# Adding gathered rows in pairs within their buffer, and ordering strided writes by stripe, in a recommendation model's kernel

## The chip, the core and the metric

The kernel runs on one core of a Trainium2 chip. The core has five engines, each with its own queue of instructions: TensorE (PE in the profile, its weight loads PEld), VectorE (DVE), ScalarE (ACT), GpSimd (POOL) and SyncE (SP, which here only issues DMAs). They run side by side and are ordered against one another by semaphores. Data lies in SBUF and PSUM on the core, both with 128 partitions, and in HBM outside it. The metric is the device time of one execution in microseconds (us); lower is better.

## The reference

The model scores 16384 rows. For each row it averages 32 word embeddings of 300 numbers and three sets of 20 embeddings of 64 numbers, looks up four single embeddings, puts all of it side by side (748 numbers) and sends it through three layers and a sigmoid. A "wide" sum of one number for each small lookup is added before the sigmoid.

```python
tok = word_emb[token_idx].mean(axis=1)          # 50000 x 300, 32 lookups a row
e1 = emb_mh1[mh1_idx].mean(axis=1)              # 1000 x 64, 20 lookups
e2 = emb_mh2[mh2_idx].mean(axis=1)              # 5000 x 64, 20 lookups
e3 = emb_mh3[mh3_idx].mean(axis=1)              # 10000 x 64, 20 lookups
o1, o2, o3, o4 = emb_oh1[oh1_idx], emb_oh2[oh2_idx], emb_oh3[oh3_idx], emb_oh4[oh4_idx]
emb = concatenate([tok, e1, e2, e3, o1, o2, o3, o4], axis=1)
wide = ...                                      # sum of one number of each of the 64 small lookups
h = relu(emb @ W1 + b1)                         # 748 -> 1024
h = relu(h @ W2 + b2)                           # -> 512
h = relu(h @ W3 + b3)                           # -> 256
return sigmoid(h @ Wd + bd + wide)
```

## The kernel before

The 16384 rows are 128 tiles of 128 rows, one row to a partition. Three kinds of work are done for each tile.

**Token rows.** The word table stays in HBM. For each of a tile's 32 tokens GpSimd issues one indirect DMA (`gather`, line 220) that fetches 128 rows of 300 floats. Two gathers fill one buffer of the ring `tok_rows` (`TOK_GROUP` = 2, `TOK_BUFS` = 3), and such a group of two rows is added up by VectorE two groups later (`TOK_LAG` = 2). `add_up` (line 525) does it: the first group of a tile (q = 0) is one add of the two rows `a` and `b` into `tok_sum`, 300 columns of the PSUM bank `own`; each of the other 15 groups is two adds, first `a` to `tok_sum`, then `b`. The last add of a tile writes to the tile's feature row in SBUF, `g`, in place of `tok_sum`. The generator `tokens` (line 538) issues the gathers of one group and the adds of an earlier one in one go. A gather into a buffer waits until both of its rows have been added.

**Small tables.** These are done as counting and matrix products. For 6 positions at a time, 11 steps for a tile, VectorE compares keys to numbers and writes one-hot rows (`one_hots`, line 599, tile `hot`), of which ScalarE scales one part in place; TensorE multiplies them into counts in PSUM (`counts`, line 616, tile `pc`), and ScalarE evicts the counts into the tile `cnt`. An eviction writes for each of 138 table slices the 6 positions of its step, so that the 11 evictions of a tile write interleaved columns of `cnt`, a stripe each. In the next tile's steps TensorE multiplies `cnt` by the tables (`small_sums`, line 639, tile `pg`), and VectorE reduces the result into `g`.

**Layers.** Each tile's `g` is transposed by TensorE and scaled into `x` by VectorE; four tiles at a time go through the layers (`mlp`, line 798), in 32-bit floats, and ScalarE applies bias and ReLU.

The order of the work is written by hand in the loop over `n_steps` = 128 x 11 + 27 steps. Each step issues the next one-hots, the counts, a share of the small sums, the tokens due by `tokens_by` (a steady pace, some 1.4 groups a step) and a share of the layers. Every engine takes its instructions in that order.

**How waits come about.** No instruction is sent to an engine directly. `Queue` and `Program.record` (line 146) note for each one which parts of which tiles it reads and writes (`region`, line 137: first and last partition, first and last byte of a row), find the earlier instructions whose regions overlap where one of the two writes, and keep of these the last for each stream (an engine's queue, or a DMA lane). An instruction of the same engine counts too, other than on TensorE. What is known to be done already by way of an earlier wait is dropped. `emit` (line 231) then sends all of it out: one wait rides on the instruction itself, and further ones become instructions of their own, issued ahead of it (line 247). A write takes out of the list those earlier accesses that lie wholly within its region. Line 98 is where all engine calls are recorded, so that nearly every instruction bears that line, and line 222 is the gather.

A region is one span of bytes. Two evictions that write interleaved columns of `cnt` overlap as spans though they share no byte, so that each one waits for the one before it.

Of the kernel before, what the change touches and what calls it, by code (L numbers as in the profile page):

```python
# [62 lines left out]
TOK_AT = 7 * ROW  # L63
WIDE_AT = COLUMN["o4"]
G_COLS = TOK_AT + TOK_D
# [38 lines left out]
class Program:  # L104
# [31 lines left out]
    @staticmethod  # L136
    def region(ap):
        size = SIZES[ap.dtype]
        pitch = size_of(ap.tensor)
        at = int(ap.offset) * size  # L140
        p0, b0 = divmod(at, pitch)
        dims = [(int(step), int(n)) for step, n in ap.ap]
        span = sum((n - 1) * abs(step) for step, n in dims[1:])
        return p0, p0 + dims[0][1], b0, b0 + (span + 1) * size

    def record(self, emit, sequencer, stream, reads, writes, clear=(), batch=None):
        ins = Instruction(emit, sequencer, self.stream(stream))
        if batch is not None:
            batch.append(ins)
            ins.batch = batch  # L150
        needed = {}

        def need(other):
            other = other.batch[-1]
            if other.batch is ins.batch:
                return
            if other.stream == ins.stream and stream == "PE":
                return
            best = needed.get(other.stream)
            if best is None or best.tick < other.tick:  # L160
                needed[other.stream] = other

        regions = [(self.region(ap), ap.tensor.name, False) for ap in reads if on_chip(ap)]
        regions += [(self.region(ap), ap.tensor.name, True) for ap in writes if on_chip(ap)]
        for (p0, p1, b0, b1), name, write in regions:
            for (q0, q1, c0, c1, wrote, _), other in self.accesses.get(name, {}).items():
                if (write or wrote) and p0 < q1 and q0 < p1 and b0 < c1 and c0 < b1:
                    need(other)
            if name in self.taken and not write and sequencer != "PE":
                banks, bank = self.taken.pop(name)  # L170
                banks.free.append(bank)
        for other in clear:
            need(other)
        known = self.known[sequencer]
        waits = [o for s, o in needed.items() if known.get(s, 0) < o.tick]
        waits = [
            o
            for o in waits
            if not any(d is not o and d.knows(o.stream) >= o.tick for d in waits)
        ]  # L180
        if waits:
            known = dict(known)
            for o in waits:
                for s, tick in o.known.items():
                    if known.get(s, 0) < tick:
                        known[s] = tick
                known[o.stream] = max(known.get(o.stream, 0), o.tick)
                o.signals = True
            self.known[sequencer] = known
        ins.waits = waits  # L190
        self.ticks[ins.stream] += 1
        ins.tick = self.ticks[ins.stream]
        ins.known = known
        self.members[ins.stream].append(ins)
        for region, name, write in regions:
            p0, p1, b0, b1 = region
            held = self.accesses.setdefault(name, {})
            if write:
                for key in [
                    k for k in held if p0 <= k[0] and k[1] <= p1 and b0 <= k[2] and k[3] <= b1  # L200
                ]:
                    if held[key] is not ins:
                        del held[key]
        for region, name, write in regions:
            self.accesses[name][(*region, write, ins.stream)] = ins
        self.program.append(ins)
        return ins
# [62 lines left out]
def size_of(tensor):  # L270
    n = 1
    for d in list(tensor.shape)[1:]:
        n *= int(d)
    return n * SIZES[tensor.dtype]


def on_chip(ap):
    return ap.space in (bass.MemoryType.SB, bass.MemoryType.PSUM)
# [37 lines left out]
def kernel(  # L316
# [21 lines left out]
    nc = tc.nc  # L338
# [8 lines left out]
    for f in SMALL:  # L347
        n = -(-tables[f].shape[0] // P)
# [4 lines left out]
    core, nc = nc, program  # L353
# [59 lines left out]
    tok_sum = own[:, 128 : 128 + TOK_D]  # L413
# [9 lines left out]
    at = 0  # L423
# [90 lines left out]
    def features(t):  # L514
        if t not in g_of:
            g_of[t] = gp.next()
        return g_of[t]

    tiles_all = B // P
    n_groups = N_TOK // TOK_GROUP  # L520
    n_all = B // P * n_groups + TOK_LAG
    summed = set()
    token_indices = {}

    def add_up(t, q, rows):

        a, b = rows
        if q == 0:
            nc.vector.tensor_add(tok_sum, a, b)
        else:  # L530
            nc.vector.tensor_add(tok_sum, tok_sum, a)
            to = tok_sum
            if q == n_groups - 1:
                to = features(t)[:, TOK_AT:G_COLS]
                summed.add(t)
            nc.vector.tensor_add(to, tok_sum, b)

    def tokens():

        under_way = []  # L540
        for n in range(n_all):
            if n < n_all - TOK_LAG:
                t, q = divmod(n, n_groups)
                it = token_indices[t // NSUB][:, t % NSUB, :].bitcast(U32)
                tok_rows, batch = tokp.next(), []
                rows = []
                for r in range(TOK_GROUP):
                    j = q * TOK_GROUP + r
                    rows.append(tok_rows[:, r * TOK_D : (r + 1) * TOK_D])
                    program.gather(f"gather{tokp.slot}", rows[-1], word, it[:, j : j + 1], batch, tok_rows)  # L550
                under_way.append((t, q, rows))
            if n >= TOK_LAG:
                add_up(*under_way.pop(0))
            yield 1
# [373 lines left out]
    for step in range(n_steps):  # L928
        t, i = divmod(step, STEPS)
# [29 lines left out]
        if waiting and step >= waiting[0][0]:  # L959
            _, k, ks = waiting[0]  # L960
# [91 lines left out]
```

## Time and profile before

| | before |
|---|---|
| median of 3 runs | 6906.27 us (6901.63 to 6929.64) |
| the profiled execution, by itself | 6980.96 us |
| its span, first to last instruction | 6979.1 us |
| mean granted TensorE clock | 0.882 |
| TensorE matmul busy | 5500.9 us (79%) |
| GpSimd busy | 3887.4 us (56%) |
| VectorE busy | 3573.1 us (51%) |
| ScalarE busy | 2698.0 us (39%) |

Busy times are unions of an engine's instructions. Ends of matmuls are modelled, so TensorE's busy share says little on its own. Rows name an instruction by engine, operation and tiles as out<-in, with buffer numbers left out: `own<-own,tok_rows` is an add of a gathered row to the token sum, `cnt<-pc` a count eviction, `hot<-own,sc` the making of one-hots (the numbers to compare with lie in the bank `own` too), `tok_rows<-in_word_emb_dram,it` a gather. "[5.48 <-DVE own]" behind a row is idle time of its engine ahead of it and what ended it. "remote" or "another core or an unknown queue" stands where a semaphore rose and no instruction that the profile shows ended just before; "issue" where nothing was waited for.

### The profile page before, as it was taken

The page shows a single profiled execution, that of the slowest core. Times are in us where ns is not written, and L with a number is a line of the kernel's source. Part 1 is how long each engine was busy: PE and PEld are TensorE (multiplying, and loading weights), DVE is VectorE, ACT ScalarE, POOL GpSimd, SP SyncE. Part 2 cuts the span into 40 slices and gives each one's busy share as a digit, 9 for nine tenths or more (in the row PEclk, how much of TensorE's full clock was granted, in tenths as well). Part 3 has the DMA queues.
Part 4 walks back from the last instruction along what each step waited for, and adds up shares of the span by engine and source line. Part 5 has one row for each costly group of instructions (what it writes and reads, how often), then busy time and mean ns, then how long its engine had stood idle before and what let it go on. Part 6 is the DMA issues. An engine that isn't in the chain of part 4 may idle for free.

```text
span 6979.1 us, 84734 instructions
## 1 busy us (share of the span) xinstructions
PE 5500.9 (79%) x33626; PEld 3574.2 (51%) x33626; DVE 3573.1 (51%) x6612; ACT 2698.0 (39%) x3433; POOL 3887.4 (56%) x4103
## 2 busy tenths in 40 slices
PE   5577888878878878878878878877877887777887
PEld 3455555455455545555545545544444544444666
DVE  4555555555555555555555555555555555555541
ACT  4343433333333433343333433333333333333331
POOL 5555555555555555555555555555555555555553
PEclk8789888888989889989888988898888988889888
DMA  5333333333333333333333333333333333333331
GB/s 157 95 95 93 93 97 94 91 92 92 96 93 94 93 92 93 93 94 93 93 92 94 94 93 93 92 92 92 91 93 91 94 93 92 93 91 95 89 86 50
DMA packets 253077, 651.47 MB, mean 93 GB/s; under 512 B 119195, under 2 KB 119835, under 8 KB 252679
## 3 DMA queue, kind: packets, MB, share of 16 engines
q0 software_dynamic: 196608, 629.41, 33.4%
q1 hardware_dynamic: 56071, 16.65, 1.1%
q8 instruction: 262, 4.29, 0.3%
q14 instruction: 136, 1.11, 0.1%
HBM read 645.59 MB, written 0.07 MB: 93 GB/s over the span
## 4 chain that ended last, share of the span: by engine, by line
PE 48%; another core or an unknown queue 17%; DVE 15%; issue 14%; ACT 3%; DMA 2%; POOL 1%; DVEq 0%; SPq 0%; POOLq 0%
PE ph L98 21%; PE pg L98 19%; PE pc L98 8%; DVE own L98 7%; DVE hot L98 6%; DMA tok_rows<-in_word_emb_dram,it 2%; DVE g L98 1%; POOL tok_rows L222 1%; ACT cnt L98 1%; ACT hot L98 1%; ACT odd L98 0%; DVE keys L98 0%; DVE x L98 0%; DVE ix L98 0%
## 5 line engine op out<-in xcount | busy, mean ns | idle before, releaser
L222 POOL DMA_INDIRECT tok_rows<-in_word_emb_dram,it x4096 | 3886.5, 949 | 3009.8 <-DVE own L98 1930.3
L98 PE MATMUL pg<-terms,cnt 128*128 128x195 bf16 x17664 | 2030.6, 268 | 562.3 <-issue 352.8
L98 PEld LDWEIGHTS pg<-terms,cnt 128*128 128x128 fp8e3 x17664 | 1681.7, 106 | 850.3 <-issue 528.6
L98 DVE TENSOR_TENSOR own<-own,tok_rows 128x300 f32<-128x300 f32 x3712 | 1766.3, 476 | 583.8 <-DMA tok_rows<-in_word_emb_dram,it 457.0
L98 ACT ACTIVATE cnt<-pc 128x828 uint16<-128x828 f32 (+1 forms) x1408 | 1187.7, 844 | 1909.6 <-remote 1152.1
L98 ACT ACTIVATE hot<-hot 64x768 bf16<-64x768 bf16 (+1 forms) x1408 | 1155.2, 820 | 1780.5 <-DVE hot L98 1495.3
L98 DVE TENSOR_TENSOR hot<-own,sc 128x1656 bf16<-128x1656 bf16 (+1 forms) x1408 | 1389.0, 987 | 861.4 <-remote 531.6
L98 PE MATMUL ph<-x,w_sb 128*128 128x512 f32 (+5 forms) x3492 | 1594.9, 587 | 69.5 <-issue 34.7
L98 PEld LDWEIGHTS pc<-hot 128*128 128x128 bf16 x8192 | 622.6, 102 | 1200.5 <-issue 793.5
L98 PE MATMUL pc<-hot 128*128 128x138 bf16 x8192 | 814.2, 233 | 457.4 <-ACT hot L98 215.0
L98 PE MATMUL ph<-odd,w_sb 128*128 128x512 f32 (+2 forms) x2368 | 1061.4, 576 | 44.4 <-issue 33.7
L98 DVE TENSOR_REDUCE g<-pg 128x130 f32<-128x390 f32 (+1 forms) x512 | 260.7, 509 | 1493.2 <-remote 971.3
L98 PEld LDWEIGHTS ph<-x,w_sb 128*128 128x128 f32 (+1 forms) x3492 | 635.5, 207 | 497.6 <-issue 443.2
L98 PEld LDWEIGHTS ph<-odd,w_sb 128*128 128x128 f32 x2368 | 422.7, 204 | 313.9 <-issue 297.7
L98 PE MATMUL pc<-ident,g 128*128 128x128 f32 x762 | 150.2, 345 | 262.6 <-ACT cnt L98 188.5
L98 ACT ACTIVATE odd<-ph,b_sb 128x512 f32<-128x512 f32 (+2 forms) x365 | 231.0, 633 | 294.0 <-remote 168.1
L98 PE MATMUL ph<-even,w_sb 128*128 128x512 f32 (+2 forms) x592 | 263.7, 573 | 23.8 <-issue 16.4
L98 PEld LDWEIGHTS pc<-ident,g 128*128 128x128 f32 x762 | 111.3, 177 | 286.5 <-ACT cnt L98 207.2
L98 DVE TENSOR_TENSOR x<-pc,scale 128x768 f32<-128x768 f32 x127 | 120.8, 951 | 158.7 <-PE pc L98 88.6
L98 ACT ACTIVATE even<-ph,b_sb 128x512 f32<-128x512 f32 (+2 forms) x148 | 93.1, 630 | 170.3 <-remote 104.7
L98 PEld LDWEIGHTS ph<-even,w_sb 128*128 128x128 f32 x592 | 107.4, 205 | 98.4 <-issue 84.6
L98 DVE COPY sc<-pc 128x512 bf16<-128x512 bf16 x64 | 44.1, 690 | 175.2 <-PE pc L98 141.8
(50 smaller groups left out, 552.7 us busy)
## 6 DMA issues: line engine op xcount, KB each, us to landing
tok_rows<-in_word_emb_dram,it POOLq DMA_INDIRECT x4096
ix<-in_idx_dram SPq DMA_DIRECT2D x64, 64.0 KB
w_sb<-in_W_dram SPq DMA_DIRECT2D x6, 512.0 KB
it<-in_idx_dram SPq DMA_DIRECT2D x64, 32.0 KB
w_sb<-in_W_dram SPq DMA_DIRECT2D x1, 2048.0 KB
odd<-in_mh_dram SPq DMA_DIRECT2D x3, 682.5 KB
even<-in_mh_dram SPq DMA_DIRECT2D x1, 682.5 KB
out_dram<-x SPq DMA_DIRECT2D x29, 2.0 KB
```

What stands on the lines that cost most here:

```text
L98: lambda: call(*args, **operands), self.name, self.name, aps + list(named.values()), outs
L222: return self.nc.gpsimd.indirect_dma_start(out=out, out_offset=None, in_=table, in_offset=bass.IndirectOffsetOnAxis(ap=index, axis=0),)
```

## The change

`add_up` forms the pair's sum first: for q > 0 the rows of a group are added in place, `a = a + b` within the gathered buffer in SBUF, and then `a` is added to `tok_sum`. It is still two adds a group. The choice of the place that the last add writes to (`to`) moves up.

`region` also gives a stripe, where an access has more than one free dimension: the period of the outermost one and the bytes within a period that the access touches. In `record`, two accesses whose stripes have the same period and no common byte (`apart`) aren't ordered against each other. A write takes an earlier access off the list only if its own stripe covers it (`covers`). An access in one unbroken piece has no stripe and is treated as before.

```diff
--- before.py
+++ after.py
@@ -141,7 +141,23 @@
         p0, b0 = divmod(at, pitch)
         dims = [(int(step), int(n)) for step, n in ap.ap]
         span = sum((n - 1) * abs(step) for step, n in dims[1:])
-        return p0, p0 + dims[0][1], b0, b0 + (span + 1) * size
+        stripe = (0, 0, 0)
+        free = [(step, n) for step, n in dims[1:] if n > 1]
+        if len(free) > 1 and all(step > 0 for step, _ in free):
+            outer = max(free)
+            width = 1 + sum((n - 1) * step for step, n in free if (step, n) != outer)
+            at = b0 % (outer[0] * size)
+            if at + width * size <= outer[0] * size:
+                stripe = (outer[0] * size, at, at + width * size)
+        return p0, p0 + dims[0][1], b0, b0 + (span + 1) * size, stripe
+
+    @staticmethod
+    def apart(one, other):
+        return one[0] == other[0] > 0 and (one[2] <= other[1] or other[2] <= one[1])
+
+    @staticmethod
+    def covers(one, other):
+        return not one[0] or one[0] == other[0] and one[1] <= other[1] and other[2] <= one[2]
 
     def record(self, emit, sequencer, stream, reads, writes, clear=(), batch=None):
         ins = Instruction(emit, sequencer, self.stream(stream))
@@ -162,10 +178,11 @@
 
         regions = [(self.region(ap), ap.tensor.name, False) for ap in reads if on_chip(ap)]
         regions += [(self.region(ap), ap.tensor.name, True) for ap in writes if on_chip(ap)]
-        for (p0, p1, b0, b1), name, write in regions:
-            for (q0, q1, c0, c1, wrote, _), other in self.accesses.get(name, {}).items():
+        for (p0, p1, b0, b1, one), name, write in regions:
+            for (q0, q1, c0, c1, two, wrote, _), other in self.accesses.get(name, {}).items():
                 if (write or wrote) and p0 < q1 and q0 < p1 and b0 < c1 and c0 < b1:
-                    need(other)
+                    if not self.apart(one, two):
+                        need(other)
             if name in self.taken and not write and sequencer != "PE":
                 banks, bank = self.taken.pop(name)
                 banks.free.append(bank)
@@ -193,11 +210,14 @@
         ins.known = known
         self.members[ins.stream].append(ins)
         for region, name, write in regions:
-            p0, p1, b0, b1 = region
+            p0, p1, b0, b1, stripe = region
             held = self.accesses.setdefault(name, {})
             if write:
                 for key in [
-                    k for k in held if p0 <= k[0] and k[1] <= p1 and b0 <= k[2] and k[3] <= b1
+                    k
+                    for k in held
+                    if p0 <= k[0] and k[1] <= p1 and b0 <= k[2] and k[3] <= b1
+                    and self.covers(stripe, k[4])
                 ]:
                     if held[key] is not ins:
                         del held[key]
@@ -525,15 +545,15 @@
     def add_up(t, q, rows):
 
         a, b = rows
+        to = tok_sum
+        if q == n_groups - 1:
+            to = features(t)[:, TOK_AT:G_COLS]
+            summed.add(t)
         if q == 0:
-            nc.vector.tensor_add(tok_sum, a, b)
+            nc.vector.tensor_add(to, a, b)
         else:
-            nc.vector.tensor_add(tok_sum, tok_sum, a)
-            to = tok_sum
-            if q == n_groups - 1:
-                to = features(t)[:, TOK_AT:G_COLS]
-                summed.add(t)
-            nc.vector.tensor_add(to, tok_sum, b)
+            nc.vector.tensor_add(a, a, b)
+            nc.vector.tensor_add(to, tok_sum, a)
 
     def tokens():
```

## The prediction

> **What bounds the kernel now.** The page comes first: the busy line says whether one engine sets the pace, the chain line whose work ended last.
>
> ```profile
> span 6979.1 us, 84734 instructions
> ...
> PE 5500.9 (79%) x33626; PEld 3574.2 (51%) x33626; DVE 3573.1 (51%) x6612; ACT 2698.0 (39%) x3433; POOL 3887.4 (56%) x4103
> ...
> PE 48%; another core or an unknown queue 17%; DVE 15%; issue 14%; ACT 3%; DMA 2%; POOL 1%; DVEq 0%; SPq 0%; POOLq 0%
> PE ph L98 21%; PE pg L98 19%; PE pc L98 8%; DVE own L98 7%; DVE hot L98 6%; DMA tok_rows<-in_word_emb_dram,it 2%; DVE g L98 1%; POOL tok_rows L222 1%; ACT cnt L98 1%; ACT hot L98 1%; ACT odd L98 0%; DVE keys L98 0%; DVE x L98 0%; DVE ix L98
> ```
>
> No engine is full. The chain is half TensorE, and VectorE, the engine that the change touches most, has 15% of it; the token adds (own) have 7%. ScalarE's count evictions (cnt) have 1%. The timeline of a short stretch in the middle shows how the engines take turns.
>
> ```profile
> 3495.79 0.41 PE L98 MATMUL pc<-hot 128*128 128x138 bf16 x4
> ...
> 3497.24 0.22 PE L98 MATMUL pc<-hot 128*128 128x138 bf16 x1 [1.05 <-issue]
> ...
> 3497.95 0.23 PE L98 MATMUL pc<-hot 128*128 128x138 bf16 x1 [0.49 <-issue]
> 3500.78 0.86 ACT L98 ACTIVATE cnt<-pc 128x828 uint16<-128x828 f32 x1 [6.47 <-remote]
> 3500.94 0.56 DVE L98 TENSOR_REDUCE g<-pg 128x130 f32<-128x390 f32 x1 [7.32 <-remote]
> 3501.42 1.01 DVE L98 TENSOR_TENSOR hot<-own,sc 128x1656 bf16<-128x1656 bf16 x1
> ...
> 3502.35 2.01 DVE L98 TENSOR_TENSOR own<-own,tok_rows 128x300 f32<-128x300 f32 x4
> ...
> 3503.60 0.95 POOL L222 DMA_INDIRECT tok_rows<-in_word_emb_dram,it  x1 [5.48 <-DVE own L98]
> ...
> 3504.26 0.95 DVE L98 TENSOR_TENSOR x<-pc,scale 128x768 f32<-128x768 f32 x1
> ```
>
> TensorE comes to a crawl at 3495.79 (single matmuls, 0.7 us and more apart, that wait for nothing shown), ScalarE and VectorE stand idle for 6 to 7 us, GpSimd runs out of row buffers and waits 5.48 us. Then VectorE works off its arrears without a pause: reduce, one-hot, two groups of adds, evictions. The change does nothing for the first phase. It can only shorten the second, and only where TensorE is short of what VectorE makes. These two views price both sides of that:
>
> ```profile
> L98 DVE TENSOR_TENSOR own<-own,tok_rows 128x300 f32<-128x300 f32 x3712 | 1766.3, 476 | 583.8 <-DMA tok_rows<-in_word_emb_dram,it 457.0 <-issue 44.8 <-DVE hot L98 4.5
> L98 DVE TENSOR_TENSOR hot<-own,sc 128x1656 bf16<-128x1656 bf16 (+1 forms) x1408 | 1389.0, 987 | 861.4 <-remote 531.6 <-PE pc L98 281.4 <-issue 19.9
> ...
> L98 DVE TENSOR_TENSOR own<-tok_rows 128x300 f32<-128x300 f32 x128 | 60.7, 474 | 38.3 <-DMA tok_rows<-in_word_emb_dram,it 31.9 <-issue 3.6 <-DVE g L98 0.4
> L98 DVE TENSOR_TENSOR g<-own,tok_rows 128x300 f32<-128x300 f32 x128 | 60.2, 470 | 4.4
> ```
> ```profile
> POOL tok_rows L222 <- DVE own L98: 1930.3, 1019, 20.4
> ...
> DVE own L98 <- DMA tok_rows<-in_word_emb_dram,it: 488.9, 459, 3.8
> ```
>
> Adds busy: 1766.3 + 60.7 + 60.2 = 1887 us. On the chain they have 7% of 6979 us, 489 us. So about 489/1887 = 26% of what an add costs is on the path: the share by which I weigh savings on VectorE.
>
> **The change part by part.** *Waits that go.* The standalone waits of the program all stand under line 247:
>
> ```profile
> L247 DVEq EVENT_SEMAPHORE  x1886: 21/21/21, 13.1 to 6900.0; - x189
> L247 ACTq EVENT_SEMAPHORE  x1096: 17/17/38, 9.9 to 6766.5; - x183
> ```
>
> A group's first add needs its gather and the add before it, two semaphores, so one wait is an instruction of its own. The new pair add reads only the gathered buffer and needs the gather alone; the second add needs the pair add alone (same engine, later tick). So up to 15 of 16 groups x 128 tiles = 1920 lose a wait; nearly all of VectorE's 1886 fit that. The other 128 (q = 0) keep theirs. Mostly the sequencer does such a wait while VectorE still runs the instruction before it: the one-hot ends at 3501.42 + 1.01 = 3502.43 and the adds behind it begin at 3502.35, 0.08 us earlier. There the 21 ns cost nothing. They show where VectorE has run dry and waits for a landing, as in the chain in order of time:
>
> ```profile
> 3508.55 0.47 DVE own L98
> 3509.02 0.03 issue
> 3509.05 0.48 DVE own L98
> 3509.53 0.67 issue
> 3510.20 0.02 DVEq L247
> 3510.22 0.04 issue
> 3510.26 0.49 DVE own L98
> 3510.75 0.02 issue
> 3510.78 0.48 DVE own L98
> ```
>
> From the end of the standalone wait's own time to the add it is 0.06 us, where an add that holds its wait follows 0.02 to 0.03 us behind its releaser. So 0.04 us for each of 459 landings waited for: 18 us of VectorE.
>
> *The order of dependence.* Before, every add depends on the one in front, also from group to group: 0.03 us between them. In the four adds of 2.01 us that is 4 x 0.476 = 1.90 plus three gaps of 0.03. After, the first add of a group is independent of the add before it, and an independent instruction starts early: 0.08 us before the end (one-hot to adds), 0.10 us (adds to x: 3502.35 + 2.01 = 3504.36 against 3504.26). Each place where two groups follow directly gains 0.03 + 0.09 = 0.12 us. How many such places? 2048 groups and 1408 one-hots, so at least 640 groups have no one-hot in front; some of these, up to 459, waited for a landing instead. Between 181 and 640; I take 400, near the middle: 400 x 0.12 = 48 us (22 to 77). Inside a group the second add still depends on the first: 0.03 us, as now.
>
> By the Trainium skill (VectorE: DVE Perf Modes, The DRAIN you can't avoid) the next operation doesn't start until the pipe is empty, and in a chain of copies semaphores between them cost nothing extra; these 48 us would be nil. The two overlaps above speak against its use here (the section allows that operations which aren't held start earlier).
>
> *The add itself.* Out of PSUM into PSUM 476 ns; two rows in SBUF into PSUM 474; PSUM and a row into SBUF 470. The new form, SBUF and SBUF into SBUF, stands nowhere at this size; between "no change" and a few ns shorter I take 470, the SBUF-output row: 1920 x 6 ns = 12 us (0 to 20).
>
> VectorE together: 18 + 48 + 12 = 78 us (about 40 to 115). On the path 26%: 20 us.
>
> *What the new form takes from GpSimd.* A two-SBUF-input add exists in the trace, once a tile (q = 0):
>
> ```profile
> 161.66 0.94 POOL L222 DMA_INDIRECT tok_rows<-in_word_emb_dram,it  x1 [0.30 <-issue]
> ...
> 162.86 0.47 DVE L98 TENSOR_TENSOR own<-tok_rows 128x300 f32<-128x300 f32 x1
> 162.91 1.23 POOL L222 DMA_INDIRECT tok_rows<-in_word_emb_dram,it  x1 [0.30 <-issue]
> ```
> ```profile
> L222 POOL DMA_INDIRECT tok_rows<-in_word_emb_dram,it x4096: 941/949/1233, 3.2 to 6897.1; - x196
> ...
> L98 DVE TENSOR_TENSOR own<-tok_rows x128: 467/470/532, 9.8 to 6842.1; 128x300 f32<-128x300 f32 x128
> ```
>
> The gather that starts just behind that add takes 1.23 us instead of 0.95, and the longest such add 532 ns instead of 470: each holds the other up, by at most 284 and 62 ns. This is what the Trainium skill says (SBUF — State Buffer, Who interferes with whom): a VectorE instruction with two SBUF inputs contends with a GpSimd instruction that reads SBUF. The trace agrees, at 1.23 against 0.95 us. After the change 1920 adds are of this form, up from 128. An unrelated add covers a gather's start in about 0.47 of every 0.949 + 0.30 = 1.25 us, 38%, and holds it up by half of 0.284 on average: 1920 x 0.38 x 0.14 = 102 us of GpSimd (0 to 545). GpSimd waits 1930 us for buffers, which hides most. It shows where VectorE waits for landings: DMA and POOL have 3% of the chain, 209 us; two gathers in 2.5 us get 0.05 longer, 2%, so 4 us on the path. The most would be 0.284 for each of 459 landings, 130 us.
>
> *Count evictions on ScalarE.* Each now writes its own stripe of cnt and doesn't wait for the eviction before it. That one lies behind it in the same queue, with a one-hot scaling between, and is long done: only the wait instruction goes, at most 1096 x 17 ns = 19 us of an engine that is busy 39%. ScalarE's 3% of the chain makes it below 1 us. What hides it is ScalarE's waiting for TensorE (6.47 us above); without that cover it would cost its 19 us. The readers of cnt still wait for the last eviction, and other strided tiles (x, g, hot) keep a partner with another stride or none, so their waits stay.
>
> No queue is reordered and no DMA added. A buffer comes free with the second add, as now. No wait is added; the q = n_groups - 1 branch only moves.
>
> *Sum.* 20 saved on VectorE, 4 given to GpSimd, ScalarE 0: 16 us, 0.2%. The profiled execution took 6980.96 us (6979.1 of span and 1.9 around it), 75 above the median of 6906.27; terms of this size are the same for both. 6981 becomes 6965, the median 6890.
>
> **The rivals.** *Everything lands on the path.* If VectorE's arrears are what TensorE waits for after every crawl, all 78 us count: 6828. For it: the chain names only the last releaser, and adds ahead of a one-hot in VectorE's queue delay it whole. Against: VectorE is idle half of the time. Between the two lie 6820 to 6860.
>
> *Nothing to be had.* Without the early start of independent adds, 30 us are left on VectorE, 8 on the path, less 4 for GpSimd: 6902. The same comes out if the waits don't go as I read the code, or if TensorE, its granted clock 0.88 on average,
>
> ```profile
> core 0: 6979.1 us, clock 0.882
> ```
>
> takes longer crawls when it is fed sooner. The crawl that waits for nothing speaks for it; that the chain holds adds at all, against.
>
> *Slower: the gathers become the bound.* Pair adds are released by landings, in step with the next gathers, so they might meet nearly always. Gathers of 1.23 us come to 4096 x (1.23 + 0.30) = 6270 us, near the whole span, and the landings that VectorE waits for come later. All 459 at 284 ns: 6906 - 20 + 130 = 7016; at half of that 6951. It decides from 56 us on, 0.12 us for each landing, a mean gather of about 1.01 us. For it: the row at 162.91. Against: 1930 us of slack, and most of the 128 present adds leave no mark, as the median of 949 ns with a far maximum shows.
>
> **How the numbers follow.** 0.5% is 35 us, about what a measurement of this kernel can tell from no change: below 6872 is faster, above 6941 slower. My case (6860 to 6905) 0.50, of which a fifth lies below 6872; all on the path 0.23; nothing to be had (6900 to 6925) 0.17; gathers 0.10. Faster 0.23 + 0.10 = 0.33, slower 0.10, same 0.57. The range 6825 to 6930 leaves out the gather case and the far end of the full gain.
>
> **What would show it.** Right: standalone waits of VectorE down from 1886 to some 200 and of ScalarE by most of 1096; pairs of groups in VectorE's timeline that begin before the add in front ends; own plus tok_rows adds near 1875 us busy; the chain's adds below 7%. Wrong: the mean gather above 1.0 us with more waiting on landings (gathers), the gap between groups still 0.03 us (nothing to be had), or the share of TensorE's crawls ("another core or an unknown queue") much changed, for which I have no step.

## The result and the profile after

| | before | after |
|---|---|---|
| median (20 runs each) | 6914.65 us (6883.58 to 6929.99) | 6885.76 us (6859.82 to 6917.88) |
| ratio | | 0.9964 (95% interval 0.9952 to 0.9977) |
| span of the profiled execution | 6979.1 us | 6891.5 us |
| granted clock in it | 0.882 | 0.874 |

The change gains 25 us (16 to 33), 0.36%. That is by the ratio of the table; the medians themselves lie 29 us apart. The two profiled executions lie further apart than the medians (88 us), so differences between their times don't measure the change; counts and durations in them do. The head of the page, with the chain of waits:

```profile
span 6891.5 us, 81907 instructions
...
PE 5525.6 (80%) x33626; PEld 3592.2 (52%) x33626; DVE 3527.7 (51%) x6612; ACT 2694.8 (39%) x3433; POOL 3909.3 (57%) x4103
...
PE 50%; another core or an unknown queue 13%; DVE 13%; issue 12%; POOL 5%; DMA 5%; ACT 2%; SPq 0%; DVEq 0%
PE pg L98 23%; PE ph L98 20%; PE pc L98 7%; POOL tok_rows L242 5%; DMA tok_rows<-in_word_emb_dram,it 5%; DVE hot L98 4%; DVE own L98 3%; DVE tok_rows L98 3%; DVE g L98 2%; ACT hot L98 1%; ACT cnt L98 1%; DVE x L98 0%; DVE keys L98 0%; ACT o
```

VectorE is busy 45 us less (3573.1 before), and gathers with their landings have 10% of the chain instead of 3%. The standalone waits (line 247 is 267 now):

```profile
L267 DVEq EVENT_SEMAPHORE  x147: 21/21/21, 54.7 to 6767.3; - x147
...
L267 ACTq EVENT_SEMAPHORE  x8: 17/38/38, 21.1 to 328.6; - x8
```

From 1886 and 1096 to 147 and 8: the waits have gone as intended. The groups of adds (count, then busy us and mean ns, then idle time ahead):

```profile
L98 DVE TENSOR_TENSOR tok_rows<-tok_rows 128x300 f32<-128x300 f32 x1920 | 889.6, 463 | 522.3 <-DMA tok_rows<-in_word_emb_dram,it 469.4 <-issue 49.8
L98 DVE TENSOR_TENSOR own<-own,tok_rows 128x300 f32<-128x300 f32 x1792 | 856.5, 478 | 62.0
...
L98 DVE TENSOR_TENSOR own<-tok_rows 128x300 f32<-128x300 f32 x128 | 60.6, 474 | 36.1 <-DMA tok_rows<-in_word_emb_dram,it 32.5 <-issue 1.2
L98 DVE TENSOR_TENSOR g<-own,tok_rows 128x300 f32<-128x300 f32 x128 | 60.2, 470 | 4.4
```

A pair add takes 463 ns where the adds to the token sum took 476 on average. All adds together went from 1887 to 1867 us. VectorE's timeline shows two groups that follow directly:

```profile
3424.87 1.01 DVE L98 TENSOR_TENSOR hot<-own,sc 128x1656 bf16<-128x1656 bf16 x1
3425.79 0.46 DVE L98 TENSOR_TENSOR tok_rows<-tok_rows 128x300 f32<-128x300 f32 x1
3426.29 0.48 DVE L98 TENSOR_TENSOR own<-own,tok_rows 128x300 f32<-128x300 f32 x1
3426.67 0.46 DVE L98 TENSOR_TENSOR tok_rows<-tok_rows 128x300 f32<-128x300 f32 x1
```

The second pair add starts at 3426.67, 0.10 us before the add ahead of it ends (3426.29 + 0.48 = 3426.77); before the change 0.03 us passed between them. Of the 595 pair adds that stand right behind another group's adds, 347 start before those end, by 0.09 us in the median. What it costs GpSimd (min, median, max in ns of a gather):

```profile
L242 POOL DMA_INDIRECT tok_rows<-in_word_emb_dram,it x4096: 940/946/1917, 3.1 to 6811.5; - x196
```

The median is 3 ns below the one before (949). The longest gather, 1917 ns, is a single one that starts 0.14 us into a 0.91 us memset of VectorE (at 134.76 us) and so is none of the pair adds'; all others stay below 1240. But 179 gathers take over 1000 ns where 22 did.

### The profile page after: what moved, and what is told of

Its sections match the earlier page's. It is cut to its first block, busy times and chain, and to the rows that moved or that the text cites. A ratio compares the mean times of both kernels' runs of the same rounds, so it can differ in the third digit from the quotient of the medians.

```text
span 6891.5 us, 81907 instructions
## 1 busy us (share of the span) xinstructions
PE 5525.6 (80%) x33626; PEld 3592.2 (52%) x33626; DVE 3527.7 (51%) x6612; ACT 2694.8 (39%) x3433; POOL 3909.3 (57%) x4103
## 4 chain that ended last, share of the span: by engine, by line
PE 50%; another core or an unknown queue 13%; DVE 13%; issue 12%; POOL 5%; DMA 5%; ACT 2%; SPq 0%; DVEq 0%
PE pg L98 23%; PE ph L98 20%; PE pc L98 7%; POOL tok_rows L242 5%; DMA tok_rows<-in_word_emb_dram,it 5%; DVE hot L98 4%; DVE own L98 3%; DVE tok_rows L98 3%; DVE g L98 2%; ACT hot L98 1%; ACT cnt L98 1%; DVE x L98 0%; DVE keys L98 0%; ACT odd L98 0%
## 5 line engine op out<-in xcount | busy, mean ns | idle before, releaser
L242 POOL DMA_INDIRECT tok_rows<-in_word_emb_dram,it x4096 | 3908.4, 954 | 2902.4 <-DVE own L98 1629.1
L98 PE MATMUL pg<-terms,cnt 128*128 128x195 bf16 x17664 | 2118.7, 273 | 879.4 <-issue 486.9
L98 PEld LDWEIGHTS pg<-terms,cnt 128*128 128x128 fp8e3 x17664 | 1715.5, 108 | 1186.6 <-issue 664.6
L98 PE MATMUL ph<-x,w_sb 128*128 128x512 f32 (+5 forms) x3492 | 1568.4, 579 | 42.8 <-issue 26.1
L98 PEld LDWEIGHTS pc<-hot 128*128 128x128 bf16 x8192 | 640.5, 104 | 1051.6 <-issue 722.0
L98 DVE TENSOR_TENSOR tok_rows<-tok_rows 128x300 f32<-128x300 f32 x1920 | 889.6, 463 | 522.3 <-DMA tok_rows<-in_word_emb_dram,it 469.4
L98 DVE TENSOR_TENSOR own<-own,tok_rows 128x300 f32<-128x300 f32 x1792 | 856.5, 478 | 62.0
L98 PE MATMUL pc<-ident,g 128*128 128x128 f32 x762 | 121.1, 299 | 65.1 <-ACT cnt L98 47.2
```

The lines of the kernel that those rows point to most:

```text
L98: lambda: call(*args, **operands), self.name, self.name, aps + list(named.values()), outs
L242: return self.nc.gpsimd.indirect_dma_start(out=out, out_offset=None, in_=table, in_offset=bass.IndirectOffsetOnAxis(ap=index, axis=0),)
```

## The experiments

Twelve runs follow, each beside the kernel before on the same chip. They met four chips of two kinds, which have to be kept apart: on one the granted clock is about 0.88, as in the result, and the kernel before takes 6913 to 6969 us; on the other three it is about 0.98, and the same kernel takes 5215 us. Which one a run got wasn't chosen.

### Where the clock is granted at 0.98

**adds_only** orders strided writes as before and keeps the pair adds:

```diff
-                    if not self.apart(one, two):
-                        need(other)
+                    need(other)
...
-                    and self.covers(stripe, k[4])
```

> The changed kernel with the old ordering of strided writes: adds in pairs, evictions ordered as before. My theory (the whole gain comes from VectorE's adds, the evictions' waits were covered): the full gain, ratio to the kernel before 0.996 to 0.997, some 1090 standalone waits back on ScalarE, about 150 on VectorE. Rival (the freed evictions bring the gain, by way of ScalarE): ratio 1.000.

Measured: 5234.87 us, ratio 1.0032 (1.0019 to 1.0044). Slower, which neither theory had.

**stripes_only** takes the adds back and keeps the stripes:

```diff
-            nc.vector.tensor_add(a, a, b)
-            nc.vector.tensor_add(to, tok_sum, a)
+            nc.vector.tensor_add(tok_sum, tok_sum, a)
...
+            nc.vector.tensor_add(to, tok_sum, b)
```

> The adds as before the change, the ordering by stripe kept: some 10 standalone waits on ScalarE, about 1890 on VectorE. My theory: no change, ratio 1.000 within 0.001 (below 1 us of ScalarE's 19 us lies on the path). Rival (evictions): 0.996 to 0.997.

Measured: 5217.79 us, 1.0002 (0.9993 to 1.0011). The freed evictions are worth nothing here.

**pair_waits** gives each pair add the dependence that the old first add had:

```diff
-            nc.vector.tensor_add(a, a, b)
+            program.record(
+                lambda: core.vector.tensor_add(a, a, b), "DVE", "DVE", [tok_sum, a, b], [a]
+            )
```

> The changed kernel, but each pair add is made to wait for the add before it as well, as the first add of a group did: same adds in the same places, two waits each. Groups that follow directly should again be 0.03 us apart, and the standalone wait on the landing is back. My theory (early start 48 us and landing waits 18 us of VectorE make the gain; the shorter add only 12 to 25 us): ratio 0.999 to 1.000. Rival (the add within SBUF is what is cheaper, waits cost nothing): 0.996 to 0.997.

Measured: 5248.12 us, 1.0056 (1.0042 to 1.007). It has the waits of stripes_only and differs from it by the pair add alone; so the pair add itself costs 0.54% here. Neither forecast had it slower.

**half_adds** leaves the pair adds out:

```diff
-            nc.vector.tensor_add(a, a, b)
```

> The changed kernel without the pair adds (for q > 0 only row a goes into the token sum, so 15 of 32 rows of each sum are left out; all gathers stay). It takes 1920 adds of 463 ns and a 0.03 us step each off VectorE, some 950 us, and all two-SBUF-input adds but 128. It measures what share of VectorE's time lies on the path. My theory, 26%: about 245 us less, ratio 0.960 (0.945 to 0.975). Rival (everything that VectorE does is on the path): 5940 us, 0.86. Rival (VectorE is covered by TensorE): 0.996, as the changed kernel.

Measured: 5203.7 us, 0.9975 (0.9964 to 0.9986). Some 880 us less for VectorE to do bring 13 us, far from the 245 of my theory: here it isn't VectorE that leads.

What leads is seen on the pages of the profiles. The head of stripes_only, its chain, then its gathers:

```profile
span 5216.5 us, 83646 instructions
...
PE 4865.5 (93%) x33626; PEld 3268.4 (63%) x33626; DVE 3582.4 (69%) x6612; ACT 2684.6 (51%) x3433; POOL 3879.0 (74%) x4103
...
DMA 32%; POOL 28%; DVE 15%; issue 14%; PE 11%; ACT 0%; DVEq 0%; POOLq 0%; SPq 0%
...
L242 POOL DMA_INDIRECT tok_rows<-in_word_emb_dram,it x4096 | 3878.1, 947 | 1279.2 <-issue 762.5
```

The same rows of pair_waits:

```profile
span 5247.2 us, 83646 instructions
...
L242 POOL DMA_INDIRECT tok_rows<-in_word_emb_dram,it x4096 | 3907.3, 954 | 1282.5 <-issue 796.8
```

TensorE is busy 93% and still has only 11% of the chain; gathers and their landings have 60%. The idle time ahead of gathers is 1279/4096 = 0.31 us each, hardly more than the 0.30 that passes between any two. GpSimd waits for next to nothing else (4.3 us at the longest): 3878 + 1279 = 5157 of 5216 us. So one us more of gathers should be one us more of time. Pair_waits has 29.2 us more of them and a span 30.7 us longer.

**change_again** is the change itself on such a chip.

> The changed kernel itself, beside the kernel before on this job's chip. Two regimes are known by now: granted clock 0.88 with TensorE crawling (the result, 0.9964), and granted clock 0.98 without crawls, where gathers lead the chain. My theory now (what the pair adds take from GpSimd is paid in full where gathers lead): at 0.98 ratio 1.003, as adds_only, mean gather 4 ns longer; at 0.88 again 0.996. Rival (adds_only was slower for the evictions it left ordered): at 0.98 1.000 or below.

Measured: 5230.37 us, 1.003 (1.0018 to 1.0041). Its span, chain and gathers:

```profile
span 5235.5 us, 81907 instructions
...
POOL 43%; DMA 18%; issue 16%; DVE 13%; PE 9%; ACT 0%; SPq 0%; POOLq 0%
...
L242 POOL DMA_INDIRECT tok_rows<-in_word_emb_dram,it x4096 | 3903.5, 953 | 1274.6 <-issue 1011.3
```

Gathers have 25.4 us more than in stripes_only, idle time 4.6 less, and the span is 19 longer. Not all of it is the pair adds': land_on_add, below, has none of them and a mean gather of 949 ns in its profiled execution. A place where it happens, in the timeline of change_again:

```profile
1016.84 0.46 DVE L98 TENSOR_TENSOR tok_rows<-tok_rows 128x300 f32<-128x300 f32 x1
1016.92 1.21 POOL L242 DMA_INDIRECT tok_rows<-in_word_emb_dram,it  x1 [0.30 <-DVE hot L98]
...
1018.43 0.94 POOL L242 DMA_INDIRECT tok_rows<-in_word_emb_dram,it  x1 [0.30 <-issue]
```

The gather that starts 0.08 us into a pair add takes 1.21 us, the next 0.94.

**land_on_add** has the old adds, the stripes, and of two waits lets the one on the landing ride on the add:

```diff
+        waits.sort(key=lambda o: self.in_order[o.stream])
```

> Adds as before the change, no pair adds; evictions by stripe; where an instruction has two waits, the one on a DMA rides on the instruction and the other becomes the standalone one. It tells the wait on the landing from the form of the add. My theory: at 0.98 the gain that pair_waits lost against adds_only (0.24%) without the pair add's price: ratio 0.997 to 0.998, mean gather unchanged at 947 ns; at 0.88 0.999 to 1.001, since groups that follow directly lose 0.07 us each and landings gain as much. Rival (the rider makes no difference): 1.000 in both.

Measured: 5215.57 us, 1.0002 (0.9993 to 1.0011). The rival is right: the 0.04 us at each landing are worth nothing where gathers lead. The 0.24% between pair_waits and adds_only was no gain of the waits, then, but again gathers, 954 ns against 951. In pair_waits the pair adds hold up more of them (175 against 102, in the table below); why they meet more of the gathers' starts wasn't tried.

**mixed** has pair adds only behind another group's adds, and land_on_add's line:

```diff
+        waits.sort(key=lambda o: self.in_order[o.stream])
...
+            last = program.members[program.stream("DVE")][-1]
+            if last is tok_add[0]:
+                nc.vector.tensor_add(a, a, b)
+                nc.vector.tensor_add(to, tok_sum, a)
+            else:
+                nc.vector.tensor_add(tok_sum, tok_sum, a)
+                nc.vector.tensor_add(to, tok_sum, b)
```

> Pair adds only where a group follows directly on another's adds (some 590 of 1920), elsewhere row a and row b go to the token sum one after the other with the wait on the landing riding on the add. My theory: at 0.98 the pair adds' price falls to a third (0.54% to 0.17%) and the waits' gain stays: ratio 0.999 (0.997 to 1.000); at 0.88 the early start is kept: 0.996 to 0.997. Rival (the price isn't a matter of how many pair adds there are): at 0.98 1.003.

Measured: 5216.51 us, 1.0003 (0.9994 to 1.0012), with gathers as in stripes_only:

```profile
span 5214.2 us, 83051 instructions
...
L243 POOL DMA_INDIRECT tok_rows<-in_word_emb_dram,it x4096 | 3877.6, 947 | 1277.9 <-issue 981.3
```

595 pair adds instead of 1920 leave no mark: the price is a matter of how many there are and where. (The gain of the waits that my 0.999 held isn't seen either.) The traces bear this out gather by gather. A gather that is held up takes over 1 us, and all but one to three of these in each trace start while an add with two SBUF inputs still runs. Their excess is what they take above the median gather of their trace; by how much it exceeds that of stripes_only, as a share of 5216 us, comes near the time lost:

| at 0.98 | pair adds | gathers over 1 us | their excess, us | excess over that of stripes_only | time over that of stripes_only |
|---|---|---|---|---|---|
| stripes_only | 0 | 12 | 2.3 | | |
| land_on_add | 0 | 13 | 1.9 | 0.00% | 0.00% |
| mixed | 595 | 28 | 5.1 | 0.05% | 0.01% |
| change_again | 1920 | 97 | 18.7 | 0.31% | 0.28% |
| adds_only | 1920 | 102 | 19.2 | 0.32% | 0.30% |
| pair_waits | 1920 | 175 | 33.7 | 0.60% | 0.54% |

**sums3_old** and **sums3_new** give gathers slack on such a chip, by more work on TensorE:

```diff
+                    for again in range(3):
+                        nc.tensor.matmul(
...
+                            start=(h == h0 and again == 0),
+                            stop=(h == h1 - 1 and again == 2),
```

> The kernel before with each matmul of the small sums issued three times into the same accumulator (the small features come out threefold; no other engine has more work): 35328 matmuls more, by 0.08 us some 2.8 ms more of TensorE. It makes TensorE lead also where the clock is granted at 0.98, so that gathers have slack. It is the base for sums3_new: some 6500 to 7500 us, ratio to the kernel before 1.25 to 1.45 at a granted 0.98.

> The changed kernel with the same threefold sums. My theory (the pair adds' price on GpSimd is only paid where gathers lead, the gain only comes where VectorE's arrears hold TensorE up): against sums3_old 0.996 to 1.0005, with the mean gather longer all the same by 3 to 6 ns. Rival (the change is slower on any chip that grants 0.98, whatever leads): 1.003 against sums3_old.

Measured: 7835.24 us (1.5023, 1.5002 to 1.5043) and 7838.84 us (1.5031, 1.501 to 1.5051): new against old 1.0005, within the intervals. The rival's 1.003 isn't there. The chain and the gathers of sums3_old, then the gathers of sums3_new:

```profile
PE 95%; DMA 2%; DVE 1%; POOL 1%; issue 1%; ACT 0%; DVEq 0%; SPq 0%; POOLq 0%
...
L222 POOL DMA_INDIRECT tok_rows<-in_word_emb_dram,it x4096 | 3876.0, 946 | 3901.2 <-DVE own L98 2828.7
```
```profile
L242 POOL DMA_INDIRECT tok_rows<-in_word_emb_dram,it x4096 | 3913.8, 956 | 3871.9 <-DVE own L98 2621.8
```

38 us more of gathers (10 ns each, where I had 3 to 6) vanish in 3900 us of waiting for buffers. Nor is there a gain: VectorE's adds are covered as well where TensorE has 95% of the chain. My guess of 6500 to 7500 us for the base was low; a repeated matmul cost 2620/35328 = 0.074 us, near the 0.08, on a base in which TensorE already had less room than I took.

### Where it is granted at 0.88

**pair_waits_again**, the same kernel:

> pair_waits once more, for a chip that grants 0.88 if this job meets one: what is open is which part of the change made the 0.36% there. There: early start and landing waits undone, so by my sum only the shorter add is left on VectorE (25 us, 6 of them on the path, less 4 for gathers): 0.999 to 1.000; if the shorter add or the evictions made the gain: 0.996 to 0.997. At 0.98: 1.0055 as before, with the mean gather 7 ns longer, which by 4096 gathers is 29 us.

Measured: 6956.78 us, 0.9986 (0.9973 to 0.9999) beside 6969.44. That lies between the two forecasts, and its interval doesn't decide between them. Here the kernel is not slower, though its gathers are the longest of all:

```profile
L242 POOL DMA_INDIRECT tok_rows<-in_word_emb_dram,it x4096 | 3935.6, 961 | 2941.9 <-DVE own L98 1684.9
```

**half_adds_again**:

> half_adds once more (no pair adds, 15 of 32 rows of each sum left out), for a chip that grants 0.88: what share of VectorE's time lies on the path where TensorE crawls. By 26%: some 245 us less than the changed kernel, ratio to the kernel before 0.960. If the chain's share overstates it: 0.975 to 0.99. At 0.98: 0.9975 as before.

Measured: 6763.08 us, 0.9789 (0.9766 to 0.9812) beside 6913.38, as the second forecast had it. Its busy line:

```profile
PE 5430.8 (80%) x33626; PEld 3543.8 (52%) x33626; DVE 2683.1 (40%) x4692; ACT 2700.0 (40%) x3433; POOL 3879.2 (57%) x4103
```

VectorE has 3527.7 - 2683.1 = 845 us less than in the changed kernel, and the time is (0.9964 - 0.9789) x 6913 = 121 us less (103 to 139), with the changed kernel's ratio taken from the result. So 121/845 = 14% (12 to 16) of VectorE's time lies on the path, and that with the pair adds' hold on GpSimd taken away too. The clock wasn't the same, either: these executions were granted 0.886 to 0.891, the kernel before beside them 0.877 to 0.881. No run tells what the clock alone would have brought, so 14% may be too high.

**mixed_again**:

> mixed once more (pair adds only where a group follows directly on another's), for a chip that grants 0.88. If the early start of pair adds behind another group's adds makes the gain: 0.996 to 0.998, with no loss at 0.98 (1.0003 there), a version that is never slower. If the shorter add or the single wait everywhere makes it: 0.999 to 1.000.

Measured: 6916.26 us, 0.9999 (0.9986 to 1.0012) beside 6913.38. It has the early starts of the changed kernel (356 pair adds begin before the adds ahead of them end, against 347), the freed evictions and the landing's wait on the add; together they don't show.

## Why the prediction was right, and where its sum was not

*The direction and the time.* 16 us were forecast and 25 (16 to 33) measured. The case that I put first came about: a small gain through VectorE's adds, within 0.5%.

*Standalone waits.* Right as to the count (some 200 were forecast on VectorE, 147 remain). The evictions' waits were rated at nothing, and stripes_only shows it at 0.98. At 0.88 this part wasn't run alone, but mixed_again holds it and gains 0.01% (-0.12 to 0.14).

*The early start.* Right as to the mechanism and near in size on VectorE: 0.09 us before the end instead of 0.03 after it, in 347 places where 400 were taken, some 42 us instead of 48. In the time it isn't seen: mixed_again has as many early starts, and less than 10 us of gain. The Trainium skill says (VectorE: DVE Perf Modes, The DRAIN you can't avoid) that in a chain of copies the semaphores cost nothing extra. These adds don't agree: one that waits for the add ahead follows 0.03 us behind it, an independent one starts 0.09 us early.

*The add itself.* 463 ns, 13 below the mean of 476 and not 6. But the second adds, at 478, lie 2 ns above that mean, so that all adds together lost 20 us (1887 to 1867), near the upper end of the 0 to 20 that I gave.

*The price on GpSimd.* The hold-up is as forecast: a gather that starts just behind the start of a pair add takes 1.21 us instead of 0.94. The Trainium skill says (SBUF — State Buffer, Who interferes with whom) that a VectorE instruction with two SBUF inputs contends with a GpSimd one that reads SBUF. The trace agrees, at 1.21 against 0.94 us. The sum was too high, 102 us forecast against 3908.4 - 3886.5 = 22 us (32 if only the gathers over 1 us are counted, 36 against 4). The 38% was too much: 476 gathers start during an add with two SBUF inputs, where it gives some 730. And only 177 of these take over 1 us; those that start with less than 0.14 us of the add left aren't held up at all. On the result's chip the slack took it up, as forecast. That the chain there gives gathers and landings 10% instead of 3% is not this price: mixed_again, with a third of the pair adds, has 11%, and pair_waits_again, with all of them and the most gathers held up, 5%. I had given the gathers' becoming the bound 10%, against 1930 us of slack. At 0.98 there is no such slack, and that rival comes true with gathers of 953 ns, far below the 1.01 us that I named; the point from which it decides is not the length of a gather but whether GpSimd waits for anything.

*The step that failed: the 26%.* I weighed VectorE's savings by the adds' share of the chain over their busy time. Half_adds_again measures 14%. With it, 18 + 42 + 20 = 80 us of VectorE (the 18 as forecast; no run shows them by themselves) come to 11 us, less than was measured. So the forecast lies near the result partly by luck: a weight that was too high made up for something that the sum lacks.

*What stays open.* 25 us (16 to 33) stand against 11. The short adds with old waits (pair_waits_again) have 0.14% (0.01 to 0.27), the early starts with a third of the short adds (mixed_again) 0.01% (-0.12 to 0.14), all of it together 0.36% (0.23 to 0.48). The intervals are too wide to share the gain out; it could also be that the first few us taken from VectorE are worth more than the average of 845. The 0.36% was measured on one chip, and the change itself wasn't run again where 0.88 is granted. The prediction also named a sign of being wrong, a much changed share of the crawls, and that share went from 17% to 13%. The execution of before that was profiled took 6981 us, more than any of the 20 runs, and the other kernels at 0.88 have 14 to 15%, so this doesn't decide. No run settles where the gain comes from.

## What to carry to other kernels

Before an operand is moved, ask who else uses the way to it: an add with two inputs in SBUF was 13 ns shorter here and held up gathers by up to 0.3 us. The change that brought 1920 of them gained 0.36% on a chip where the gathers had slack, and lost 0.3% where they had none. Read whether an engine has slack from its idle time per instruction (0.31 us against the 0.30 that is always there meant none), not from its busy share: GpSimd was at 74% in stripes_only and had none. A share of the chain says what is on the path, not what an equal saving would bring: taking a piece of work out altogether measures that on average, and the granted clock has to be read beside it.

## What the runs showed of the hardware

The same kernel took 5215 us on chips that granted a clock of 0.98 and 6914 us on one that granted 0.88, a third more for a tenth less clock. The profile of before shows that the clock alone isn't the measure: TensorE's crawls with 0.7 us from one instruction to the next, and 17% of the chain with no releaser. In the stretch from 3495 to 3502 us, which holds the crawl that the prediction shows, the mean granted clock is 0.97. At 0.98 the chain of change_again has no such share at all. What sets the crawls off, no run here tells. On the chips without them the bound is one engine's row of 4096 gathers at 0.947 + 0.31 = 1.26 us each, 5150 us in all; half_adds, with some 880 us less for VectorE, gained 13.
